# Second layer of a four-layer network: weights and router logits moved into the first layer, the map passes with a PSUM operand, the shared experts as a chain of their own, expert rows added before they are transposed

## The chip, the cores and the metric

The kernel runs on one core of a Trainium2 chip. A core has five engines with queues of their own: TensorE (PE in the profile; its weight loads are listed as PEld), VectorE (DVE), ScalarE (ACT), GpSimd (POOL) and SyncE (SP, which here only issues DMAs). The metric is the device time of one execution in microseconds; lower is better. All arithmetic is fp32.

## What is computed

The network has four layers. Each does `x = x + s * silu(g)`, where s comes from an attention block and g from a feed-forward block, both fed with the layer norm xn of x. There are 8 batches of 512 tokens with 128 features. The change is in the second layer (L1): its s is an RWKV-like recurrence, its g a mixture of experts.

```python
# attention: k, v, r from xn mixed with xn shifted by one token
k = k_in @ Wk;  v = v_in @ Wv;  r = sigmoid(r_in @ Wr)
# per batch and feature, over the 512 tokens:
max_out = maximum(mx, ck + tf)
out = (exp(mx-max_out)*num + exp(ck+tf-max_out)*cv) / (exp(mx-max_out)*den + exp(ck+tf-max_out))
...                                      # mx, num, den decay with td
s = (r * out) @ Wo

# feed-forward: 2 shared experts for every token, and the best 2 of 8 experts
ffn(x, w1, w2, w3) = (silu(x @ w1.T) * (x @ w3.T)) @ w2.T       # 128 -> 256 -> 128
logits = xf @ router_w.T + expert_bias
rw, sel = top_k(logits, 2);  rw = softmax(rw)
g = sum over the two chosen experts of rw * ffn(xf, expert)  +  sum over 2 shared of ffn(xf)
```

The other layers are a windowed attention with a quantised feed-forward (L0), a windowed and latent attention with a phase-weight feed-forward (L2), and a large complex-valued attention with soft experts (L3). L2 needs `tw` (cosine and sine of its phase weights) and `wgg`, which are computed once.

## The kernel before, in words

Activations are kept feature-major: x, xn and s are 128 partitions x 4096 tokens. A batch is one 512-column tile. Engines run what `Net.in_order` records (line 74) in exactly the order of the program, each engine for itself; the profile gives all of these instructions line 83, so groups are told apart by tile names. What is issued without `in_order` may be put anywhere in its engine's queue by the scheduler.

The layer norm of L1 is part of the last steps of L0's feed-forward. That function's order is written out by hand in the string `L0_FFN`: a letter is a step, a number its tile. The steps that matter here are E (centre x on PE), F, G (variance), H (`row`, scaled rows on DVE, also sent to DRAM as `xrows`), I (transpose on PE) and J (`xn` copied by ACT).

After L0, `L2Consts.weights` (line 1198) makes tw and wgg for layer 2: DVE steps on `ang` and `turns`, two Sin on ACT, a small matmul. Then `l1_layer` (line 576) loads its weights by DMA (m1_w13 is 2560 KB, m1_w2 1280 KB), scales its mixing weights `wm` on DVE, and has three stages:

1. `route` (line 758). PE makes the logits `ps_lg` (32 token tiles of 128, 8 columns each), DVE finds the first and second maximum and their one-hot rows (`first_max`), PE counts tokens per expert (`ps_cnt`), and DVE turns the counts into a place for each token and choice. Then eight map passes: DVE compares the place's row with `upto` (0 to 127) to get `ob` (128 x 8 x 128), and its tile with `upto[0:72]` to get `ot` (128 x 8 x 72). POOL and DVE make the two halves of `hold` from ot (token number, gate weight), and PE sums `ps_map` from ob and hold. The result says, for each of 72 tiles of 128 rows, which token stands in each row (`source`) and with which weight. Between logits and maps, the receptances (sigmoid, `ps_mix` into s) are computed for all 8 batches.
2. `tiles` (line 898). For each pair of tiles POOL gathers token rows (`xr`, indirect DMA from xrows), PE transposes them (`tp_g`), multiplies by the pair's expert weights (`ps_ab`, chosen by a register), ACT and DVE make `hh`, PE transposes it (`tp_h`) and multiplies by w2 (`ps_y`); the rows `yy` go to `yrows` in DRAM. Between these, steps of a Python generator `attention` are taken: 19 steps per batch (mixed k and v, scans, one Exp over 128 x 2048 `ex`, four reciprocals, output product `ps_o`), 84 of them in this stage.
3. `rows_back` (line 1001). For each of 8 blocks of 512 tokens, PE computes the shared experts in four parts (`first`: pa and pb with Silu on ACT and the product h on DVE; `second`: accumulate into `acc`). POOL gathers each token's two expert rows (`yr`, 64 indirect DMAs in all); PE turns and adds them into the same accumulator by a matmul with the identity (`back`), 8 per block. Then `gated`: Silu, product with s, sum into x. Attention steps stand between the parts: 10 per block.

PSUM has eight banks. In this layer before: `a1_p` (mixed, ps_o) has 2, `f1_g`, `f1_a` and `f1_t` 2 each.

Of the kernel before, what the change touches and what calls it, by code (L numbers as in the profile page):

```python
# [224 lines left out]
def l0_attention(net, xn, s_out, p0, w, bias):  # L225
# [196 lines left out]
    "B6 I0 F5 E7 D4 J0 C6 G5 E4 F7 H3 D6 I3 F4 G7 E6 J3 G4 F6 H5 G6 I5 H7 J5 H4 I7 H6 I4 "  # L422
    "J7 J4 I6 J6 "
# [3 lines left out]
def l0_ffn(net, x, xn, s):  # L427
    nc, tc = net.nc, net.tc
    K = TB // P
    with ExitStack() as st:  # L430
# [140 lines left out]
        )  # L571
        for part in "".join(L0_FFN).split():
            parts[part[0]](int(part[1:]))


def l1_layer(net, x, xn, s_out):
# [3 lines left out]
    nc, tc = net.nc, net.tc  # L580
    with ExitStack() as st:
        p1 = st.enter_context(tc.tile_pool(name="a1_1", bufs=1))
        p2 = st.enter_context(tc.tile_pool(name="a1_2", bufs=2))
        experts = L1Experts(net, st)
        w = net.load(p1, "a1_w")
        par = net.load(p1, "a1_p")
        td = p1.tile([P, 1], F32, tag="td", name="td")
        nc.scalar.activation(td, par[:, 0:1], AF.Exp)
        nc.vector.tensor_scalar(td, td, -1.0, None, ALU.mult)
        tf = par[:, 1:2]  # L590

        rest = p1.tile([P, 3], F32, tag="rest", name="rest")
        nc.vector.tensor_scalar(rest, par[:, 2:5], -1.0, 1.0, ALU.mult, ALU.add)
        wm = p1.tile([P, 3, 2, P], F32, tag="wm", name="wm")
        for i in range(3):
            nc.vector.tensor_scalar(
                wm[:, i, 0, :], w[:, i, :], par[:, 2 + i : 3 + i], None, ALU.mult
            )
            nc.vector.tensor_scalar(
                wm[:, i, 1, :], w[:, i, :], rest[:, i : i + 1], None, ALU.mult  # L600
            )
# [9 lines left out]
        pp = st.enter_context(tc.tile_pool(name="a1_p", bufs=2, space=PSUM))  # L611
        experts.open_psum(st)
        pe, dve, act, pool = (
            net.in_order(e) for e in (nc.tensor, nc.vector, nc.scalar, nc.gpsimd)
        )

# [9 lines left out]
        def receptance(b):  # L626

            act.activation(s_out[:, ts(b, S)], mixed(2, b), AF.Sigmoid)
# [4 lines left out]
        def attend(b):  # L633
# [48 lines left out]
            dve.tensor_tensor(up, up, out, ALU.mult)  # L682
# [7 lines left out]
        def attention(batches):  # L690
            for b in batches:
                yield from attend(b)

        experts.route(xn, (pe, dve, act, pool), receptance)

        between = attention(range(B))
        experts.tiles((pe, dve, act, pool), between, 84)
        experts.rows_back(x, xn, s_out, (pe, dve, act, pool), between)


class L1Experts:
# [4 lines left out]
    def __init__(self, net, st):  # L706
        nc, tc = net.nc, net.tc
# [54 lines left out]
    def route_in(self, xn, engines, receptance, st):  # L762
# [47 lines left out]
        for b in range(B):  # L810
            receptance(b)
# [1703 lines left out]
```

## Time and profile before

| what | us |
|---|---|
| median of 3 runs (lowest, highest) | 2430.46 (2427.05, 2439.55) |
| the profiled execution, its own time | 2420.28 |
| its span in the trace | 2418.6 |
| PE, DVE, ACT, POOL busy in the span | 2224.3, 2007.3, 1842.5, 1567.8 |

The second layer lies from 403 to 777 us of the span: the first logits matmul starts at 409.57, the first map matmul at 446.36, the first expert matmul at 479.18, the first shared-expert matmul at 638.71, and layer 2's first matmul at 776.77. In a row of the profile's tables, "out<-in" names the tiles written and read; after the bar come busy time and mean duration in ns, then how long the engine stood idle before such instructions and what ended the idleness. An fp32 matmul shows as two records. A matmul's recorded duration overlaps the next one, so the spacing of starts tells its cost.

### The profile page before, as it was taken

Reading aid. Unit: us, or ns where it says so; the run is one execution under the profiler, and the core shown is the slowest. Engines: PE = TensorE matmul, PEld = TensorE weight load, DVE = VectorE, ACT = ScalarE, POOL = GpSimd, SP = SyncE. Lnnn points to the kernel's source line nnn. Section 1 sums busy time; section 2 is a strip of 40 time slices with the busy share of each in tenths; the row PEclk is TensorE's granted clock in tenths of the full one; section 3 lists DMA queues with packets and bytes.
Section 4 is the critical chain, followed back from the end, with each engine's and each line's share of the span. In section 5 each row is a group of like instructions: output and inputs, shape, how many; then the busy total and the mean of one; then the engine's idle time right before and its main releaser. Section 6 shows DMA issues by size and latency. Waiting matters only on the chain.

```text
span 2418.6 us, 49187 instructions
## 1 busy us (share of the span) xinstructions
PE 2224.3 (92%) x17826; PEld 1552.5 (64%) x17826; DVE 2007.3 (83%) x3638; ACT 1842.5 (76%) x3841; POOL 1567.8 (65%) x1422
## 2 busy tenths in 40 slices
PE   6999997689888999868999999999999999999897
PEld 4666675456434666645777777777777777777774
DVE  5577877666675888859999999999999999999474
ACT  4566664155433798947999999999999999999763
POOL 5344434364244878756688788888878878887323
PEclk7899987899999999989999999999999999999888
DMA  2000002022111000033443443344344434433000
GB/s 70 1 2 2 2 1 105 8 63 64 39 29 27 3 16 16 23 111 102 102 112 91 109 114 105 98 102 109 101 110 107 104 91 115 110 91 90 18 1 36
DMA packets 91617, 156.94 MB, mean 65 GB/s; under 512 B 20144, under 2 KB 44464, under 8 KB 91120
## 3 DMA queue, kind: packets, MB, share of 16 engines
q1 hardware_dynamic: 86880, 143.57, 22.5%
q0 software_dynamic: 4352, 8.92, 1.5%
q8 instruction: 142, 2.33, 0.4%
q10 hardware_dynamic: 144, 1.31, 0.1%
q14 instruction: 99, 0.81, 0.1%
HBM read 30.52 MB, written 12.06 MB: 18 GB/s over the span
## 4 chain that ended last, share of the span: by engine, by line
PE 52%; DVE 32%; ACT 5%; POOL 5%; issue 4%; SPq 1%; DMA 1%; POOLq 0%; ACTq 0%; DVEq 0%
PE sc L83 10%; DVE sc L83 7%; DVE y L83 5%; DVE r L83 5%; PE ps_av L83 5%; PE tp L83 4%; PE ps_u L83 4%; PE ps_kq L83 4%; PE av L83 3%; PE ps_n L83 2%; DVE mx L83 2%; PE ps_ab L83 2%; DVE e L83 2%; PE ps_mix L83 2%; PE ps_v L83 1%
## 5 line engine op out<-in xcount | busy, mean ns | idle before, releaser
L83 POOL TENSOR_TENSOR ek<-E,kn 128x512 f32<-128x512 f32 (+3 forms) x512 | 435.0, 872 | 206.7 <-DMA kn<-nr 200.6
L83 PE MATMUL sc<-r 128*128 128x512 f32 (+3 forms) x1024 | 310.1, 446 | 25.3 <-DVE y L83 22.4
L83 POOL TENSOR_TENSOR e<-e,mx 128x1024 f32<-128x1024 f32 x112 | 212.1, 1900 | 182.9 <-DVE mx L83 90.9
L83 POOL TENSOR_TENSOR r<-r,rs 128x1024 f32<-128x1024 f32 x128 | 304.7, 2381 | 21.5 <-DMA rs<-r 21.3
L83 PE MATMUL ps_av<-u,at 128*128 128x128 f32 x2560 | 306.7, 275 | 0.0
L83 PEld LDWEIGHTS ps_av<-u,at 128*128 128x128 f32 x2560 | 296.0, 192 | 0.1
L83 ACT ACTIVATE y<-y,mn 128x384 f32<-128x384 f32 (+3 forms) x512 | 288.8, 569 | 4.0 <-DVE mn L83 3.2
L83 PEld LDWEIGHTS sc<-r 128*128 128x128 f32 x1024 | 165.6, 192 | 190.2 <-issue 120.3
L83 DVE SCALAR_TENSOR_TENSOR y<-sc,qn,V 128x512 f32<-128x512 f32 (+3 forms) x512 | 246.5, 544 | 8.8
L83 DVE CUSTOM_DVE_ANT_0 y<-y,ps_g,ncs 128x384 f32<-128x384 f32 (+3 forms) x512 | 253.2, 541 | 0.0
L83 ACT ACT_TABLE_LOAD x180 | 230.9, 1283 | 10.7 <-PE ps_mix L83 4.3
L83 PEld LDWEIGHTS tp<-ident,y 128*128 128x128 f32 x1280 | 161.7, 142 | 113.3 <-issue 49.3
L83 PE MATMUL tp<-ident,y 128*128 128x128 f32 x1280 | 203.8, 274 | 1.8 <-ACT s L83 0.7
L83 ACT COPY at<-tp 128x512 f32<-128x512 f32 (+1 forms) x384 | 195.3, 509 | 7.8 <-PE tp L83 5.1
L83 DVE TENSOR_TENSOR sc<-sc,EF 128x1280 f32<-128x1280 f32 x128 | 191.9, 1499 | 4.4
L83 DVE SCALAR_TENSOR_TENSOR sc<-sc,ek 128x1280 f32<-128x1280 f32 x128 | 189.7, 1482 | 6.4 <-issue 5.0
L83 POOL TENSOR_TENSOR s<-s,o 128x512 f32<-128x512 f32 x120 | 154.2, 1285 | 32.0 <-ACT o L83 32.0
L83 ACT ACTIVATE y<-y 128x1280 f32<-128x1280 f32 x128 | 163.4, 1277 | 5.0 <-DVE y L83 4.3
L83 DVE TENSOR_TENSOR r<-sn,ps_kq 128x1024 f32<-128x1024 f32 x128 | 155.2, 1212 | 9.6 <-ACT sq L83 9.6
L83 ACT ACTIVATE sq<-ps_kq 128x1024 f32<-128x1024 f32 x128 | 131.7, 1029 | 32.7 <-PE ps_kq L83 32.7
L83 DVE TENSOR_TENSOR r<-ct,ps_kq 128x1024 f32<-128x1024 f32 x128 | 155.2, 1213 | 0.0
L83 ACT ACTIVATE e<-e 128x1024 f32<-128x1024 f32 x112 | 117.3, 1061 | 38.6 <-POOL e L83 38.2
(449 smaller groups left out, 5070.5 us busy)
## 6 DMA issues: line engine op xcount, KB each, us to landing
rs<-r SPq DMA_DIRECT2D x256, 256.0 KB, 3.7
kn<-nr SPq DMA_DIRECT2D x512, 64.0 KB, 2.0
yrows<-yy SPq DMA_DIRECT2D x36, 128.0 KB, 1.8
ct<-trig SPq DMA_DIRECT2D x16, 256.0 KB
EF<-E SPq DMA_DIRECT2D x16, 256.0 KB, 2.4
EF<-E SPq DMA_DIRECT2D x16, 192.0 KB
m_w<-m_w SPq DMA_DIRECT2D x1, 2560.0 KB
x<-x SPq DMA_DIRECT2D x8, 256.0 KB, 5.8
```

What stands on the lines that cost most here:

```text
L83: ins = op(*args, **kwargs)
```

## The change

- **Constants earlier.** A new class `L1Consts` holds L1's weights, masks and counters for the whole of L0 and L1. Four small loads (m1_r, eb, a1_w, a1_p) are issued by SP at the start; the two large ones by ACT's queue ahead of L0's attention. The scalings `wm`, `td`, `rest` are done by ACT there, and the casts of the counters by POOL.
- **Logits in L0.** `L0_FFN` gets steps L (logits of a tile, four matmuls) among its last steps and M (bias added).
- **Layer 2's weights** become a generator, taken as the last steps of `attention`.
- **Receptance** is `tanh(z/2)`; the factors are made up by `(out + 1) * up` and by a Wo scaled with 0.5. Three receptances now stand ahead of ps_cnt on PE, five behind. `a1_p` has one bank (two before).
- **Map passes.** `upto` is copied to PSUM (a bank of f1_g) and both comparisons read it there; ot is made before ob; the gate half of hold is made by ACT, eight scalings per pass. The list of experts (`past`, `ef`) is made after the passes.
- **Shared experts** are a generator `shared_steps` with 32 steps, an accumulator bank `acc` of their own, and their result kept in `sh` (128 x 4096). Four steps stand between map pass 0's operands and its matmuls, one after the maps, one behind the first gathers, eight in the tile loop, the rest in rows_back.
- **Rows** of both choices are gathered into one tile per block (two such tiles), added by DVE (`summed`), transposed by PE (four per block), then `sh` is added on DVE, and Silu and the gate follow, spread over three blocks. Attention steps: 90 in the tile loop, 8 per block afterwards.

```diff
-    "B6 I0 F5 E7 D4 J0 C6 G5 E4 F7 H3 D6 I3 F4 G7 E6 J3 G4 F6 H5 G6 I5 H7 J5 H4 I7 H6 I4 "
-    "J7 J4 I6 J6 "
+    "B6 I0 F5 E7 D4 J0 C6 G5 E4 F7 H3 D6 I3 F4 G7 E6 J3 G4 F6 H5 G6 I5 L0 L1 H7 J5 L2 H4 I7 L3 H6 I4 "
+    "J7 L5 J4 I6 L7 J6 L4 L6 M0 "
...
+        def logits(t):
+            for k in range(K):
+                i = K * t + k
+                pe.matmul(
+                    lg[:, i, :], lhsT=xn[:, ts(i, P)], rhs=router.rw, start=True, stop=True
+                )
...
+class L1Consts:
...
+    def fill(self):
+        net, nc, p1, E = self.net, self.net.nc, self.p1, self.E
+        act = net.in_order(nc.scalar)
+        self.w13 = net.load(p1, "m1_w13", act)
+        self.w2 = net.load(p1, "m1_w2", act)
...
-        pp = st.enter_context(tc.tile_pool(name="a1_p", bufs=2, space=PSUM))
+        pp = st.enter_context(tc.tile_pool(name="a1_p", bufs=1, space=PSUM))
...
-            act.activation(s_out[:, ts(b, S)], mixed(2, b), AF.Sigmoid)
+            act.activation(s_out[:, ts(b, S)], mixed(2, b), AF.Tanh, scale=0.5)
...
-            dve.tensor_tensor(up, up, out, ALU.mult)
+            dve.scalar_tensor_tensor(up, out, 1.0, up, ALU.add, ALU.mult)
...
+            yield from l2.weights(p1, lambda name: pp.tile([P, S], F32, tag="ps", name=name))
...
+    def shared_steps(self):
...
+        def first(b, n):
+            e, j = parts[n]
+            xt = self.xn[:, ts(b, TB)]
+            pa, pb = (self.p_t.tile([P, TB], F32, tag="t", name=n) for n in ("pa", "pb"))
+            pe.matmul(pa, lhsT=w13[:, e, ts(j, P)], rhs=xt, start=True, stop=True)
+            pe.matmul(pb, lhsT=w13[:, e, ts(NH + j, P)], rhs=xt, start=True, stop=True)
+            a = self.p3.tile([P, TB], F32, tag="sa_s", name="sa_s")
+            act.activation(a, pa, AF.Silu)
+            h = self.p3.tile([P, TB], F32, tag="sh_s", name="sh_s")
+            dve.tensor_tensor(h, a, pb, ALU.mult)
+            return b, n, h
+
+        def second(b, n, h):
+            e, j = parts[n]
+            if n == 0:
+                self.acc = self.p_acc.tile([P, TB], F32, tag="acc", name="acc")
+            last = n == len(parts) - 1
+            pe.matmul(self.acc, lhsT=w2[:, e, j, :], rhs=h, start=(n == 0), stop=last)
+            if last:
+                act.copy(self.sh[:, ts(b, TB)], self.acc)
+
+        waiting = None
+        for b in range(B):
+            for n in range(len(parts)):
+                made = first(b, n)
+                if waiting:
+                    second(*waiting)
+                waiting = made
+                yield
+        second(*waiting)
+        yield
...
+        upto = self.p_g.tile([P, P], F32, tag="g", name="upto_p")
+        act.copy(upto, k1.upto)
...
         dve.tensor_tensor(g2, m2, m1, ALU.subtract)
         act.activation(g2, g2, AF.Exp)
-        for b in range(B):
+
+        for b in range(3):
+            receptance(b)
+        cnt = self.p_a.tile([P, 2, NTILE * E], F32, tag="a", name="ps_cnt")
...
+        for b in range(3, B):
             receptance(b)
...
             dve.tensor_tensor(
                 ot, tl[:, cut].unsqueeze(2).to_broadcast(tshp),
-                self.upto[:, 0:NK].unsqueeze(1).to_broadcast(tshp), ALU.is_equal,
+                upto[:, 0:NK].unsqueeze(1).to_broadcast(tshp), ALU.is_equal,
+            )
+            dve.tensor_tensor(
+                ob, at[:, cut].unsqueeze(2).to_broadcast([P, N, P]),
+                upto.unsqueeze(1).to_broadcast([P, N, P]), ALU.is_equal,
             )
...
-            dve.tensor_tensor(
-                hold[:, :, 1, :], ot, val[:, cut].unsqueeze(2).to_broadcast(tshp), ALU.mult
-            )
+            for j in range(N):
+                act.activation(
+                    hold[:, j, 1, :], ot[:, j, :], AF.Copy, scale=val[:, n + j : n + j + 1]
+                )
+            held[n] = ob, hold
...
+        for n in range(0, 2 * NTILE, N):
+            hold_of(n)
             if n == 0:
+                for _ in range(self.A_SHARED - 1):
+                    next(self.shared)
+            add(n)
...
+            def summed(b):
+                dve.tensor_tensor(
+                    rows[b][:, 0], rows[b][:, 0], rows[b][:, 1], ALU.add
                 )
 
             def back(b):
-                for i in range(4 * b, 4 * b + 4):
-                    for c in range(2):
-                        pe.matmul(
-                            acc[b][:, i % 4, :], lhsT=rows.pop((i, c)), rhs=net.ident,
-                            start=False, stop=(i % 4 == 3 and c == 1),
-                        )
+                ps = self.p_g.tile([P, 4, P], F32, tag="g", name="ps_b")
+                r = rows.pop(b)
+                for i in range(4):
+                    pe.transpose(ps[:, i, :], r[:, 0, i, :], net.ident)
+                g = p2.tile([P, TB], F32, tag="sg", name="sg")
+                dve.tensor_tensor(
+                    g, ps.rearrange("p k t -> p (k t)"), self.sh[:, ts(b, TB)], ALU.add
+                )
+                act.activation(g, g, AF.Silu)
+                return g
...
+            for b in range(B + 2):
+                for n in range(3):
+                    if given < left * min(3 * b + n + 1, 3 * B - 3) // (3 * B - 3):
+                        given += 1
+                        next(self.shared, None)
+                    for _ in range(self.C_BETWEEN // 3 + (n < self.C_BETWEEN % 3)):
+                        next(between, None)
+                    if n == 0 and 1 <= b <= B:
+                        summed(b - 1)
+                    if n == 1 and 2 <= b:
+                        gated(b - 2, gs.pop(b - 2))
+                    if n == 2 and 1 <= b <= B:
+                        gs[b - 1] = back(b - 1)
+                        if b + 1 < B:
+                            gather(b + 1)
```

Here `left` is 32 minus the steps already given to the route (A_SHARED = 5) and the tile loop (B_SHARED = 8), and C_BETWEEN is 8.

## The prediction

> **What bounds the kernel now.** First the page's sums, then busy time by stage of the second layer, then the timeline of the stages' seams, then the groups of the last stage. The stages, cut where the chain changes engine (columns: stretch, its length, then busy us and count of PE, PEld, DVE, ACT, POOL, granted clock, DMA share, GB/s):
>
> ```profile
> 403.00:424.00 21.00, 15.39 (x74) 14.81 (x72) 5.59 (x23) 5.90 (x13) 1.63 (x14) 0.64 0.63 238
> 424.00:446.00 22.00, 16.23 (x36) 7.69 (x37) 18.71 (x43) 5.58 (x9) 1.71 (x1) 0.80 0.00 1
> 446.00:474.00 28.00, 17.93 (x130) 16.12 (x128) 21.94 (x23) 0.60 (x1) 11.72 (x8) 1.00 0.00 1
> 474.00:480.00 6.00, 1.85 (x4) 1.01 (x5) 0.00 (x0) 0.37 (x1) 4.64 (x5) 0.77 0.16 44
> 480.00:640.00 160.00, 147.93 (x697) 93.19 (x696) 105.45 (x191) 87.96 (x171) 70.18 (x67) 0.97 0.23 57
> 640.00:777.00 137.00, 116.67 (x352) 56.71 (x351) 88.66 (x125) 45.83 (x61) 67.22 (x64) 0.96 0.13 33
> ```
>
> The layer has 374 us of the 2418.6. PE is nearly full only in the tile loop (480 to 640). Ahead of it the router is a chain that changes engine, behind it PE and DVE wait in turn.
>
> ```profile
> 403.16 0.41 DVE L83 TENSOR_TENSOR ang<-f_w 128x256 f32<-128x256 f32 x1
> 409.57 13.79 PE L83 MATMUL ps_lg<-m_r,xn 128*128 128x8 f32 x64
> 423.40 0.42 DVE L83 TENSOR_TENSOR lg<-ps_lg,eb 128x256 f32<-128x256 f32 x1 [2.36 <-PE ps_lg L83]
> 431.55 0.42 DVE L83 COPY tot<-ps_cnt 128x256 f32<-128x256 f32 x1 [2.13 <-PE ps_cnt L83]
> ...
> 448.52 1.23 DVE L83 TENSOR_TENSOR ob<-at,upto 128x1024 f32<-128x1024 f32 x1 [1.25 <-PE ps_map L83]
> 450.56 1.65 POOL L83 TENSOR_TENSOR hold<-ot,token 128x576 f32<-128x576 f32 x1 [2.27 <-PE ps_map L83]
> 451.12 2.17 DVE L83 TENSOR_TENSOR ob<-at,upto 128x1024 f32<-128x1024 f32 x1
> ```
>
> Layer 2's weights hold 403.2 to 409.5, then the logits 13.8 us at a clock of 0.50. The ob pass takes 1.23 alone and 2.17 while POOL writes hold (450.56 to 452.21), the time that both overlap. One map pass is so 3.55 (ob 451.12, next ob 454.67).
>
> ```profile
> L83 PE MATMUL pa<-xn,m_w 128*128 128x512 f32 x64 | 34.5, 622 | 0.0
> L83 DVE TENSOR_TENSOR h<-a,pb 128x512 f32<-128x512 f32 x32 | 21.4, 671 | 28.4 <-PE pb L83 16.6 <-ACT a L83 11.8
> L83 PE MATMUL acc<-ident,yr 128*128 128x128 f32 x128 | 15.4, 275 | 0.0
> L83 DVE TENSOR_TENSOR x<-x,pr 128x512 f32<-128x512 f32 x7 | 4.8, 692 | 0.2
> ```
>
> In the last stage DVE waits 28.4 for the shared experts' product. A 512-column matmul there is two records that start 0.43 apart, 0.86; a shared step (pa, pb, acc) is 2.57 of PE.
>
> **The sum, part by part** (t is the end of the lg addition, 423.82 before).
>
> Start. The layer's constants come before layer 0. SP issues four loads earlier (0.33 + 0.42 + 0.33 + 0.52); a0_w then goes out at 12.6 for a user at 29.11, so this is covered. The two big loads go out on ACT's queue near 29 us, where the DMA share is 0.02; before, they held the DMA share near 1.0 from 408 to 418, and they are needed after 410. ACT's ten small scalings start 0.2 apart: 2.0, inside ACT's idle 29.06 to 31.18. POOL gets 2.65 or more (iotas 0.67, memsets and selects 1.04, four casts 0.94 by DVE's rows, up to 2.4 by POOL's tt cast of 0.61), and POOL is the chain until rstd at 13.64. Bounds 0 and 4.1; half of the lower sum, since the order is free: **+1.5**.
>
> Logits. After I5 (PE 401.28) PE now has L0 L1 L2 I7 L3 I4 L5 I6 L7 L4 L6. An L is 8 records, 0.13 each at full clock (ps_c), 0.215 at half: 1.04 or 1.72; an I is 0.55. The clock before stayed at 1.00 until 408.7, so I take six L at full clock and two at half: t = 413.1, bounds 412.1 and 415.7. The weights' 6.4 us go out of the way by this too: **-10.7**.
>
> Counts. This is a new wait. ps_cnt now stands behind three receptances; these share one bank (two before), and the first Tanh stands on ACT behind the gate's Exp, which waits for DVE until t+5.7. So: Exp 0.23, Tanh 0.60, mixed 1.72 at full or 3.43 at half clock (2.5), Tanh 0.6, mixed (2.0), cnt 1.8: tot at t+13.6 where it was at t+7.7. DVE's 16 small steps and the map wait behind it: **+5.9**, bounds 4.9 and 7.3 by the two clocks.
>
> The Trainium skill, "TensorE: Matmul & The Clock Gate", Part 1 (What's actually happening), says that the clock halves after one idle window of about 3.4 us and needs as long a busy one to return. Here a gap of 4.9 us (404.1 to 409.0) halved it, as the page has it, but 13.7 us of unbroken logits did not bring it back. By the page the gap of 3.6 us in front of the second receptance is a cold start, and the term would be 7.3.
>
> Map. From tot: on PE five receptances at 1.72 + 0.6 + 0.1 after the first (11.4), four shared steps (12.0, with ACT's table load of 1.28 and hold(0) ahead of the first Silu; DVE's second pass stands behind their four h, so the maps start late by them), eight passes. Per pass DVE has ot 0.75 and ob 1.21, POOL 1.65, ACT eight scalings (two gsel start 0.20 apart at 16 columns, so 0.25 at 72) 2.0, PE 16 x 0.14 = 2.23: PE sets 2.25. That the PSUM operand frees DVE from POOL no row shows outright; if not, 2.92 per pass, +5. Gathers and tp_g follow as before, over two further shared steps. into(0) starts at t+63.0 (before 479.18, tot+47.6): **+1.8**, bounds 0 and 7. So into(0) stands at 476.1, with six of 32 shared steps done.
>
> Tile loop (before 479.2 to 638.6, PE 92% busy). Eight shared steps 20.6, six attention steps of 4.29/19: 1.4. Off: the cold start (two tiles at 0.50), 2.5, and 0.5 where a step falls in PE's wait behind Exp (3.1 each): **+19**, bounds 16 and 24.
>
> Rows (before 638.6 to the last x at 778.2: 139.6). PE falls from 112 to 67: 19 shared steps 48.9, back 32 transposes for 128 records (14.2 to 3.5), attention 14. POOL's 64 gathers at 1.25 stay 80. DVE now leads: 3 batches and a rest at 16.5 each (mx 1.24, num 1.23, den 1.21, four reciprocals 3.7, thirteen of 0.67 to 0.75) 52.8; layer 2's weights 2.9; h 19 x 0.67 = 12.7; sum, add, two for the gate 8 x 2.76 = 22.1: 90.5. Its waits: for Exp 3.89 and 2.16 before, 3.0 x 3; for k 1.1 x 3. The last block, with Sin's and Silu's table loads, 3. The gathers don't decide: the first eight land 3.3 + 10 + 2.5 = 16 us into the stage, where summed(0) stands (a block and 4 us); later ones wait for the transposes two blocks back, as there are two row buffers, and POOL's 10 us a block are under DVE's 11.4 and its waits. In all 106; bounds 94 (no waits), 126 (10.8 a batch as in 691 to 725): **-33.6**.
>
> Tanh for Sigmoid and the merged gate product move table loads and 0.05 a batch: nothing, under the route's waits on PE.
>
> +1.5 - 10.7 + 5.9 + 1.8 + 19 - 33.6 = **-16.1**. The profiled execution took 2420.28 and becomes 2404.2; it lies 10.2 under the median of 2430.46, so the forecast is **2414.4**.
>
> **Rivals.**
> *Denser.* Rows at 94, tiles +16: 15 more, 2399.4. For it: layer 2's steady stage has DVE at 19.7 of 20. Against it: Exp's table loads remain.
> *Moved, not saved.* The shared steps keep their waits, the rows stage takes 126: 2434.4. For it: 28.4 us of DVE's waits belong to h, and they stood on ACT and PE, which still come first. Against it: PE's queue there is 45 us shorter.
> *The cold rows stage, slower.* With PE at 67 of 106 the gate halves the clock in the rows stage. PE then needs 134, 28 more: 2442.4. It decides from a mean clock below 67/106 = 0.63 on. For it: 424 to 432 ran at 0.50 with PE 2.5 of 8 busy. Against it: 676 to 696 kept 1.00 with PE at 14.2 of 20.
> That the change doesn't do what it says is not open for the counts of instructions; only the PSUM operand's effect is, priced above.
>
> **How the numbers follow.** Forecast 0.40 (own range 2405 to 2420), denser 0.22, moved 0.21, cold 0.17. A difference under 0.5% (12 us) can't be told from none. Faster: nearly all of the first two, 0.58. Same: 2418 to 2443 holds moved and part of the cold case, 0.25. Slower: 0.17. The range reaches to 2395 below and 2442 above.
>
> **What would show it.** ps_lg ends by 413 and no layer-2 weights stand ahead of it; tot 13 to 14 us behind lg, with Exp then Tanh as releasers; ob near 1.2 throughout and ps_map unbroken; tile loop near 178; rows stage near 106 with DVE busy about 90 and a clock over 0.9. The forecast is wrong if the rows stage stays over 120, or if the tile loop takes more than its 22 us of added PE work.

## The result, and the profile after

The changed kernel takes 2439.96 us (median of 13 runs, 2430.77 to 2444.61) where the kernel before takes 2430.01 on the same chip: a ratio of 1.0039, 95% interval 1.0022 to 1.0055. So it is slower by 0.4%, about 10 us, and the prediction of 16 us less was wrong in its sign. The profiled execution took 2444.1 us, with a span of 2441.2. It lies 4 above its median, while the profiled execution of before lies 10 under its own, so the two traces differ by 22.6 us and the medians by 10. A second trace of each, taken on other chips, has spans of 2436.6 (changed) and 2437.9 (before): whole traces scatter by more than the change is worth, so what follows compares the lengths of stages.

Behind layer 2's first `row` both traces need the same time (1637.8 and 1636.7 us), so everything happens up to there. Busy time by stage of the second layer in the changed kernel (columns: stretch, its length, then busy us and count of PE, PEld, DVE, ACT, POOL, granted clock, DMA share, GB/s; the stages are logits, counts, receptances and four shared steps, maps, first gathers, tile loop, rows):

```profile
403.00:416.00 13.00, 13.00 (x81) 12.54 (x79) 2.91 (x7) 3.80 (x6) 1.07 (x2) 0.67 0.26 81
416.00:433.00 17.00, 13.07 (x20) 5.14 (x18) 5.67 (x15) 1.91 (x4) 0.00 (x0) 0.55 0.01 1
433.00:458.00 25.00, 19.30 (x40) 7.62 (x39) 10.63 (x26) 8.62 (x18) 1.15 (x1) 0.93 0.00 0
458.00:475.00 17.00, 17.00 (x132) 16.29 (x131) 15.31 (x22) 13.86 (x56) 8.06 (x7) 1.00 0.01 2
475.00:486.00 11.00, 5.82 (x15) 2.55 (x15) 1.37 (x2) 2.52 (x5) 7.95 (x9) 0.84 0.15 42
486.00:673.00 187.00, 169.02 (x735) 103.41 (x735) 116.14 (x204) 94.90 (x180) 69.35 (x64) 0.95 0.18 47
673.00:797.00 124.00, 84.69 (x189) 35.44 (x189) 88.35 (x131) 39.36 (x58) 65.29 (x64) 0.83 0.13 36
```

The maps are now what the change wanted, PE busy in 17.00 of 17. But DVE, which was to lead the rows stage, works there for 88.35 us of 124: 36 us are waits.

The timeline at the same seams as before (start, duration, then idle time before it and what ended that):

```profile
415.25 0.42 DVE L83 TENSOR_TENSOR lg<-ps_lg,eb 128x256 f32<-128x256 f32 x1 [10.03 <-PE ps_lg L83]
432.19 0.42 DVE L83 COPY tot<-ps_cnt 128x256 f32<-128x256 f32 x1 [10.92 <-PE ps_cnt L83]
...
458.08 16.04 PE L83 MATMUL ps_map<-hold,ob 128*128 128x144 f32 x128
...
460.56 1.22 DVE L83 TENSOR_TENSOR ob<-at,upto_p 128x1024 f32<-128x1024 f32 x1
460.81 1.15 POOL L83 TENSOR_TENSOR hold<-ot,token 128x576 f32<-128x576 f32 x1 [0.73 <-ACT hold L83]
```

The lg addition stands 8 us earlier than before, tot does not: 16.9 us lie between them (8.2 before). ob takes 1.22 even while hold runs, and hold 1.15 where it was 1.65.

The groups that answer to pa and h of before (h is now called sh_s, Silu's result sa_s; busy time, mean ns, then idle time before them by releaser; over the whole layer):

```profile
L83 PE MATMUL pa<-xn,m_w 128*128 128x512 f32 x64 | 37.0, 663 | 8.9 <-ACT sa_s L83 8.9
L83 DVE TENSOR_TENSOR sh_s<-sa_s,pb 128x512 f32<-128x512 f32 x32 | 21.8, 681 | 48.2 <-ACT sa_s L83 24.7 <-PE pb L83 23.5
```

DVE's idle time in front of the shared experts' product is 48.2 us over the layer, where it was 28.4. In the rows stage alone, DVE waits for (us in total, times, longest):

```profile
DVE sh_s L83 <- ACT sa_s L83: 13.6, 8, 3.3
DVE sh_s L83 <- PE pb L83: 13.2, 3, 6.8
```

So 26.8 us, though PE's queue is shorter there; moving 13 of the 32 steps away took only 1.6 us of these waits with it (4.2 in the second trace, where they are 24.2).

### The profile page after: what moved, and what is told of

It reads as the page before. It is cut to its first block, busy times and chain, and to the rows that moved or that the text cites. A ratio compares the mean times of both kernels' runs of the same rounds, so it can differ in the third digit from the quotient of the medians.

```text
span 2441.2 us, 49058 instructions
## 1 busy us (share of the span) xinstructions
PE 2221.3 (91%) x17730; PEld 1537.6 (63%) x17730; DVE 2002.6 (82%) x3634; ACT 1862.5 (76%) x3921; POOL 1565.0 (64%) x1426
## 4 chain that ended last, share of the span: by engine, by line
PE 34%; DVE 23%; POOL 4%; ACT 4%; issue 3%; DMA 2%; SPq 1%; POOLq 0%; ACTq 0%; DVEq 0%
PE sc L83 8%; DVE sc L83 7%; DVE r L83 6%; DVE y L83 6%; PE ps_av L83 5%; PE ps_u L83 4%; PE ps_kq L83 4%; PE tp L83 3%; PE ps_n L83 2%; SPq L1975 1%; PE ps_p L83 1%; POOL ek L83 1%; DMA rs<-r 1%; POOL r L83 1%; POOL e L83 1%
## 5 line engine op out<-in xcount | busy, mean ns | idle before, releaser
L83 PE MATMUL sc<-r 128*128 128x512 f32 (+3 forms) x1024 | 311.1, 447 | 26.8 <-DVE y L83 23.7
```

Source lines behind the costliest of these rows:

```text
L83: ins = op(*args, **kwargs)
```

## The experiments

Each kernel was timed beside the kernel before on one chip; ratios are to that, with 95% intervals. The table gives stage lengths from each trace, as differences of start times: the lg addition, the cast to `source`, the first ps_ab, the last yy, the last x of layer 1, the first `row` of layer 2. The last yy stands for the end of the tile loop in all of them, since shared steps no longer mark it.

| run | ratio to before | lg to source | to ps_ab | to last yy | to last x | to row | sum |
|---|---|---|---|---|---|---|---|
| before, first trace | | 48.9 | 6.9 | 162.7 | 135.6 | 3.3 | 357.4 |
| before_again | 0.9996 (0.9976-1.0015) | 48.9 | 7.0 | 172.4 | 135.8 | 3.3 | 367.4 |
| changed, first trace | 1.0039 (1.0022-1.0055) | 58.9 | 11.4 | 190.2 | 121.1 | 7.7 | 389.3 |
| again | 1.0051 (1.0036-1.0066) | 59.0 | 11.4 | 184.4 | 118.1 | 7.7 | 380.6 |
| list_early | 1.0049 (1.0032-1.0067) | 59.1 | 9.2 | 189.2 | 118.4 | 7.7 | 383.5 |
| pa_bank | 1.0047 (1.0030-1.0063) | 60.0 | 11.3 | 184.9 | 118.4 | 7.7 | 382.4 |
| fill_late | 1.0030 (1.0011-1.0049) | 60.2 | 11.3 | 184.9 | 117.9 | 3.6 | 377.9 |
| cnt_first | 1.0057 (1.0037-1.0077) | 59.2 | 11.4 | 184.3 | 118.0 | 7.7 | 380.6 |
| late_out | 1.0014 (1.0001-1.0027) | 58.8 | 11.4 | 181.8 | 114.5 | 7.7 | 374.3 |
| attn_early | 1.0142 (1.0121-1.0164) | 56.6 | 11.4 | 224.5 | 99.6 | 7.7 | 399.7 |
| turn_add | 1.0035 (1.0020-1.0049) | 60.1 | 11.4 | 185.2 | 121.4 | 7.7 | 385.8 |
| no_head_steps | 1.0004 (0.9988-1.0021) | 45.6 | 9.4 | 183.8 | 124.1 | 7.7 | 370.6 |
| shared_late | 1.0060 (1.0034-1.0086) | 60.0 | 11.5 | 170.0 | 134.9 | 7.7 | 384.1 |
| all_late | 1.0048 (1.0031-1.0064) | 46.0 | 9.3 | 170.0 | 146.8 | 7.7 | 379.8 |
| all_late_mended | 0.9996 (0.9978-1.0014) | 46.1 | 9.4 | 168.9 | 143.4 | 3.6 | 371.3 |
| upto_sbuf | 1.0071 (1.0045-1.0096) | 62.7 | 11.3 | 186.3 | 120.5 | 7.7 | 388.6 |
| logits_last | 1.0051 (1.0032-1.0070) | 60.2 | 11.4 | 189.3 | 118.0 | 7.7 | 386.6 |
| mended | 0.9961 (0.9944-0.9978) | 46.0 | 9.3 | 185.5 | 121.2 | 3.6 | 365.6 |
| mended_banks | 0.9966 (0.9950-0.9981) | 46.0 | 9.3 | 180.5 | 119.3 | 3.6 | 358.6 |
| mended_all | 0.9957 (0.9940-0.9974) | 46.1 | 9.2 | 180.4 | 124.6 | 3.6 | 364.0 |

### Both kernels once more

> The kernel before as it is, for a second trace. If the first trace (2420.28 us, at the low end of its runs) is typical in layer 1: 355 to 360 us from the lg addition to layer 2's first row (357.4), with 49, 163 and 136 from lg to the first source cast, first ps_ab to last yy, and last yy to last x. If layer 1 was short by chance in that execution: 363 to 368. Time as before's other runs, ratio 1.000 within 0.002.

> The changed kernel as it is, so that the others are compared with it on one chip, and so that a second trace shows which of its stalls return. From the first source cast to the first ps_y it took 29.8 us in the first trace and 23.9 to 24.7 in three kernels that leave this stretch as it is; if the 5 us were of that one execution, 24 to 25 here, and 378 to 384 us from the lg addition to layer 2's first row (389.3 in the first trace). If they belong to the kernel, 29 to 30 again. Time 2428 to 2434 where the kernel before takes 2422.

The layer took 367.4 us in before's second trace, 10 more than in the first, all of it in the tile loop; the changed kernel's second trace lacks 8.7 of its first (5.8 of them in the tile loop). The other stages agree within 0.2 us for before, and within about 3 for the changed kernel. So the tile loop's length has to be compared as a range, 162.7 to 172.4 before and 184.4 to 190.2 after, and a rows stage between 118.1 and 121.1 is not told apart from the changed kernel's.

### Counts first, and the list of experts early

```diff
-        for b in range(3):
-            receptance(b)
         cnt = self.p_a.tile([P, 2, NTILE * E], F32, tag="a", name="ps_cnt")
...
-        for b in range(3, B):
+        for b in range(B):
             receptance(b)
```

> The changed kernel, with ps_cnt ahead of all eight receptances on PE (three stand ahead of it now). Theory 'counts', as in the prediction: ps_cnt's wait is on the path that sets the end; tot stands 8 us behind lg (16.6 now), the maps and all behind them come 5 to 8 us earlier, and so does the end. Rival 'PE's work is the path': DVE's operands for the first pass are ready at 441.6, but PE has eight receptances and four shared steps ahead of the maps in either order; the first pa then moves by under 2 us from 28.5 behind lg, or later if the receptances now run cold, and the time changes by under 2.

The timeline of this kernel at the lg addition, tot and the first pa:

```profile
415.38 0.42 DVE L83 TENSOR_TENSOR lg<-ps_lg,eb 128x256 f32<-128x256 f32 x1 [9.88 <-PE ps_lg L83]
423.94 0.42 DVE L83 COPY tot<-ps_cnt 128x256 f32<-128x256 f32 x1 [2.55 <-PE ps_cnt L83]
...
444.56 1.02 PE L83 MATMUL pa<-xn,m_w 128*128 128x512 f32 x2
```

tot comes 8.6 behind lg instead of 16.9, and nothing follows: the first pa stands 29.2 behind lg (28.8 in the changed kernel), and the ratio is no better. The rival holds in its outcome: eight receptances and the shared steps are ahead of the maps in either order, and the wait that the prediction priced at 5.9 us is off the path. It is not PE's work alone, though: two things cancel here. PE stands idle for 6.1 us in front of ps_cnt, and the receptances behind it run at full clock (1.00 from 424.8 to 436) where the first three of the changed kernel ran at half.

In list_early `past`, `ef` and `expert` are made right behind the first pass's operands.

> The changed kernel, with the list of experts (past, ef, expert) made behind the first map pass's operands, as before the change, and not after the last pass. Theory 'register loads': PE stands 3.1 us (482.5 to 485.5) in front of the first ps_ab because two loads of expert numbers into its registers come there, and more of them come between the first tiles; with the list made early some of them move into PE's idle time before the maps. First ps_ab then 6 to 9 us behind the source cast (11.4 in the changed kernel, 6.9 before), first ps_y 22 to 25 behind it (29.8; 19.4 before), the time 5 to 8 us below the changed kernel's. Rival 'cold seam': the stall is the gathers' latency and a PE at clock 0.58; then the first ps_ab comes no more than 3 us earlier, first ps_y too, and the time changes by under 2 us.

The first ps_ab moves up by 2.2 us, within the rival's 3, and PE's gap ahead of it falls from 3.1 to 1.0: that much the register loads cost there. The tile loop gives it back (189.2, within its range), and the time shows nothing.

### Layer 2's fills

`vw` and `gv` are filled by POOL memsets whose program text the change does not touch. In the changed kernel's timeline they stand between layer 1's last x and layer 2's first row:

```profile
796.77 0.69 DVE L83 TENSOR_TENSOR x<-x,sg 128x512 f32<-128x512 f32 x1
...
797.66 1.90 POOL L1259 MEMSET vw<- 128x2160 f32 x1 [10.72 <-PE ps_c L83]
...
803.43 1.04 POOL L83 TENSOR_TENSOR std<-var,neg_half 128x4 f32<-128x4 f32 x1
804.50 0.69 DVE L83 TENSOR_TENSOR row<-ps_c,std 128x512 f32<-128x512 f32 x1 [5.61 <-POOL std L83]
```

```diff
                 pool.tensor_tensor(self.std[n], v, net.neg_half.to_broadcast([P, K]), ALU.pow)
+                k.fill_now(pool)
```

`fill_now` holds the memsets of vw and gv and runs once.

> The changed kernel, with layer 2's fills of vw and gv (eight POOL memsets, 5.4 us) put behind the first std of layer 2. Before the change they ran at 8 to 16 us of the span; in the changed kernel they run at 797.7 to 803.1, since the memory of vw is now used in layer 1, and POOL makes the first std behind them. Theory 'memory': from the last x of layer 1 to the first row of layer 2 it is 7.0 us now and was 2.6; it becomes 2.6 to 3.2 again, and the time falls by 4 to 4.5 us, as POOL stands idle for 5.3 us behind the first std. Rival: the fills then delay kbs or vw of the first batch and the 4.4 us are given back there; the time changes by under 1.5.

In fill_late's timeline:

```profile
790.37 2.61 POOL L83 MEMSET vw<- 128x2160 f32 x3
790.43 0.69 DVE L83 TENSOR_TENSOR row<-ps_c,std 128x512 f32<-128x512 f32 x1 [1.44 <-POOL std L83]
```

From the last x to the first row it takes 3.6 us instead of 7.7, so 4.2 us come back; the ratio moves about as far (0.0021 below again's), but the two intervals overlap, so that the trace shows this gain and the time does not. That the memory of vw is reused is read from the wait (the fill waits for layer 1's end; before, it ran at 8.3 us of the span); the addresses themselves were not looked at.

### What the rows stage waits for

pa_bank: `pa` of a shared step in f1_a's banks while rows are brought back, `pb` in f1_t as it was.

> The changed kernel, with pa of a shared step in the two banks of f1_a while rows are brought back (they stand idle there); pb stays in f1_t. Theory 'two banks': pa and pb of one step fill both banks of f1_t, so PE can't begin the next step before DVE has taken h, and DVE's 26.8 us of waits in front of sh_s in this stage (13.6 for ACT's sa_s, 13.2 for PE's pb) come from that. They fall under 14, and the stage from the last yy to the last x from 121.8 to 107 to 112; the time 10 to 14 us below the changed kernel's. Rival 'the list of work on DVE and ACT': sh_s waits because Exp with its two table loads stands ahead of Silu on ACT, and PE because the reciprocals stand ahead of h on DVE; more banks move the waits to other tiles, and the stage falls by 4 at most.

PE's waits in the rows stage of pa_bank:

```profile
PE ps_o L83 <- DVE up L83: 19.0, 4, 10.6
PE acc L83 <- DVE sh_s L83: 12.1, 8, 4.1
```

The stage stays at 118.4: the rival holds. PE no longer waits in front of pa and pb, and waits instead in front of acc for DVE's h (12.1, where it was 4.4 in the changed kernel) and, above all, as before, in front of ps_o, for `up` at the end of DVE's reciprocals (15.8 in the changed kernel). What stands in PE's queue behind ps_o waits too.

```diff
-            ps = pp.tile([P, S], F32, tag="ps", name="ps_o")
-            pe.matmul(ps, lhsT=w[:, 3, :], rhs=up, start=True, stop=True)
-            act.copy(out, ps)
...
             act.copy(v, mixed(1, b))
             yield
+            product_of_last_batch()
```

`product_of_last_batch` is the three lines taken out, for the batch before; batch 7 keeps them where they were.

> The changed kernel, with ps_o of an attention batch issued behind the next batch's k and v instead of two steps behind up (the last batch's as it was). Theory 'ps_o blocks PE': in the rows stage PE stands up to 10.6 us in front of ps_o until DVE has done the reciprocals and up, with the next shared step's pa and pb behind it, and DVE then waits for pb: that is why 26.8 us of DVE's waits stand in front of sh_s. PE's wait for up falls from 16 to 19 us to under 6, DVE's waits for sh_s to under 14, and the stage from the last yy to the last x from 118 to 105 to 111; the time 7 to 13 us below the changed kernel's. Rival 'DVE's own list': what PE gains at ps_o it loses in front of acc, as h stands behind the same reciprocals on DVE; the stage falls by 3 at most.

PE's largest wait in late_out's rows stage:

```profile
PE ps_o L83 <- DVE up L83: 10.8, 1, 10.8
```

What is left in front of ps_o is the one wait of the last batch, which has no next batch to hide behind. DVE's waits for sh_s fall only to 21.5 (11.4 + 10.1; 24.2 in again), the stage to 114.5, the tile loop by 2.6 (inside its spread), and the ratio to 1.0014: 9 us less than again on the same chip, with intervals that don't touch. So ps_o was part of it; the theory's 105 to 111 for the stage is not reached, and the banks (pa waits 7.3 for sa_s) come up next. They are tried together below.

turn_add lets PE add the two rows again (eight matmuls with the identity per block, no sum on DVE).

> The changed kernel, with the two gathered rows added by PE again: per block eight matmuls with the identity into ps_b instead of DVE's sum and four transposes. So DVE has 8 x 0.68 = 5.4 us less and PE some 64 records more (3.5 to 7 us by the clock). Theory 'DVE leads the rows stage', as in the prediction: the stage from the last yy to the last x falls from 118 by 3 to 6. Rival 'waits lead it': neither DVE's 5.4 nor PE's 7 stands on the path; it changes by under 2. If it grows by 3 or more, adding on DVE was worth it.

The stage takes 121.4: 3.3 more than in again, but no more than the 121.1 of the changed kernel's first trace, and the time (1.0035 against 1.0051) doesn't part them either. It does not fall by 3 to 6, so DVE's 5.4 us of work are not what the stage hangs on; what adding on DVE is worth is not shown.

### Where shared steps and attention stand

```diff
-    B_BETWEEN = 90
+    B_BETWEEN = 128
```

> The changed kernel, with 128 steps of attention in the tile loop where it has 90, so 24 and layer 2's weights are left for the rows stage instead of 62. Theory 'rows stage follows DVE and its waits': two batches of 16.5 us of DVE and their waits for Exp and ps_o leave it: 118 to 82 to 92, held by POOL's 64 gathers at 1.25; the tile loop, bound by PE, grows by 38 steps of 4.29/19, 8.6, or up to 14 with new waits: time 12 to 25 us below the changed kernel's. Rival 'moved': the tile loop's PE waits for the denser attention as much as the rows stage sheds, or the gathers hold the rows stage at 105; the time changes by under 6.

The rows stage sheds 18.5 us and the tile loop gains 40, 1.05 per attention step where PE's work is 0.23. Neither theory holds: the loop takes more than the rows stage sheds, and the kernel is some 22 us slower than again. In the loop PE now waits 15.8 us in front of ps_ab for DVE (3.0 in the changed kernel) and 7.6 in front of ps_y for ACT (2.4), which with 8.6 of work names 27 of the 40. The tile loop is bound by PE only while its other queues are loose.

```diff
-    A_SHARED = 5
+    A_SHARED = 1
```

> The changed kernel, with one shared step in the route where it has five: none stands between the first pass's operands and the maps, and the four go to the rows stage. From the first pa to the first map matmul it took 14.0 us (10.3 of PE and a wait of 3 for Silu's table). Theory 'the rows stage has room': the maps start 31 to 33 us behind the lg addition instead of 42.9, the first source cast 47 to 49 (59.0), and the stage from the last yy to the last x grows from 118 by no more than 5 (four h of 0.68 and some waits): time 6 to 11 us below the changed kernel's. Rival 'a shared step costs as much there': with 3 us for each it grows by 12, and the time changes by under 3.

The theory holds, with both sizes a little past its ranges: 13.4 us less up to `source`, 2 less to the first ps_ab, and 3.0 to 6.0 more in the rows stage (against the changed kernel's two traces). The ratio of 1.0004 is some 10 us under the changed kernel's. A shared step ahead of the maps cost 3.8 us of the path; in the rows stage it costs 1.5 or less.

shared_late has B_SHARED = 0 instead of 8, all_late has both edits, all_late_mended also those of late_out and fill_late. With more than 21 steps left the rows stage gives one or two at each place (`while given < ...` for `if`).

> The changed kernel, with none of the shared steps in the tile loop (eight now) and 27 in the rows stage (19 now), one or two at each of its places. Theory 'the rows stage has room': from the first ps_ab to the last yy 184.4 becomes 162 to 166 (eight steps of 2.57), and the rows stage grows from 118 by 5 to 10: time 10 to 16 us below. Rival 'a shared step costs as much there': the rows stage grows by 16 to 24, as DVE waits for each sh_s, and the time changes by under 4.

> The changed kernel, with one shared step in the route and none in the tile loop, so that 31 of the 32 stand in the rows stage, nearly as before the change. Theory 'the rows stage has room': both savings add up, 12 from the route and 20 from the tile loop, against 8 to 15 more in the rows stage (118 to 126 to 133; it was 135.6 before the change): time 17 to 24 us below the changed kernel's, under that of the kernel before by 5 to 12. Rival 'a shared step costs as much there': the rows stage goes to 145 or more, and the time is within 5 of the changed kernel's.

> As all_late, with ps_o behind the next batch's k and v, and layer 2's fills behind its first std. Theory: both gains found alone (9 by the time or 6 by the trace, and 4.2) add to that of all_late: 10 to 13 us below all_late, and 15 to 25 below the kernel before. Rival: with 31 shared steps in the rows stage PE's wait for up is filled already by them, so that of the two only the fills' 4 us remain.

Here the rival holds: eight steps leave the tile loop (-14.4) and cost 16.9 in the rows stage, 2.1 each; in all_late against no_head_steps 22.7 for 13.8. The rows stage has room for four more steps, not for twelve. The mended one gains 12 us on all_late, as the theory has it, and yet only reaches the kernel before: with 31 steps there, the rows stage loses what the route and the tile loop gain.

### Two parts of the change alone

In logits_last the steps L0 to L7 follow J6 in the list, ahead of M0.

> The changed kernel, with the logits of all eight tiles behind the last step of the first layer (behind the last xn) instead of between its last steps. Theory, as in the prediction's logits term: 32 narrow matmuls then stand on the path, 8.3 us at full clock and 13.8 at half; less the 2 to 4 that stand there now: the lg addition 6 to 10 us behind where it is, and the time 5 to 9 us above the changed kernel's. Rival: the logits between the last steps delay the transposes and xn by what they take, so the place is worth nothing: time within 3.

The rival holds: ratio 1.0051, again's own. In this trace the last xn is copied at 402.1 (410.3 in the changed kernel), and the lg addition follows 9.4 us later, at 411.5 (4.9 later there): as the time is the same, logits among the last steps seem to push xn back by what they take, though single positions scatter by more than this (see the end). The trace shows one thing more. The 64 records of logits run from 401.9 to 411.4 without a gap, and in their midst the granted clock halves (stretch, its length, busy us and count by engine as above, clock, DMA share, GB/s):

```profile
402.00:406.40 4.40, 4.40 (x42) 4.40 (x41) 0.00 (x0) 1.97 (x3) 0.00 (x0) 1.00 0.36 112
406.40:411.40 5.00, 5.00 (x26) 5.00 (x25) 0.00 (x0) 0.00 (x0) 0.00 (x0) 0.50 0.00 0
```

In upto_sbuf the map passes read upto from SBUF.

> The changed kernel, with upto read from SBUF in the map passes instead of PSUM. Theory 'the PSUM operand frees DVE from POOL': ob takes about 2.2 us again where POOL's hold overlaps it (1.21 to 1.22 now), hold 1.65 on POOL (1.15 now); a pass is then 0.75 + 2.2 of DVE instead of PE's 2.0, and from the first map matmul to the source cast it takes 21 to 25 us instead of 16.1: time 5 to 8 us above the changed kernel's. Rival 'ACT taking the gate half frees it': DVE no longer makes a half of hold, and ob stays at 1.2 to 1.3; the maps stay under 18, the time within 2.

A map pass of it, and the next one's ot:

```profile
459.88 1.21 DVE L83 TENSOR_TENSOR ob<-at,upto 128x1024 f32<-128x1024 f32 x1
460.13 1.97 POOL L83 TENSOR_TENSOR hold<-ot,token 128x576 f32<-128x576 f32 x1 [0.79 <-DVE ot L83]
461.02 1.70 DVE L83 TENSOR_TENSOR ot<-tl,upto 128x576 f32<-128x576 f32 x1
```

The maps take 21.8 us instead of 16.1, as the theory has it, but the slow pass is now ot (1.70 for 0.75), since it is ot that starts while hold runs, and hold grows from 1.15 to 2.0. From lg to `source` the kernel loses 3.7 us of the 5.7, as the four shared steps ahead of the maps took 12.5 in this trace and not 14.0. The ratio of 1.0071 agrees with the theory, but its interval reaches down to again's ratio.

### The faults taken away

mended joins no_head_steps, late_out and fill_late; mended_banks adds pa_bank; mended_all also moves layer 2's weights behind batch 6.

> The changed kernel, with one shared step in the route (four moved to the rows stage), ps_o behind the next batch's k and v, and layer 2's fills behind its first std. Theory: what the three gave alone adds up, 11 (time, no_head_steps), 6 to 9 (late_out) and 4 to 5 (fill_late): 21 to 25 us below the changed kernel's 2435, which is 2410 to 2414 where the kernel before takes 2424, ratio to before 0.994 to 0.996; from lg to layer 2's first row 358 to 362 (380.6). Rival: late_out and no_head_steps fill the same PE wait, and together give 12: ratio 0.998 to 1.000.

> As mended, with pa in the two idle banks of f1_a in the rows stage. Theory 'the causes mask each other': alone the banks gave nothing, as ps_o held PE anyway; now PE's waits of 10.9 for sh_s in front of pb and 8.9 for sa_s in front of pa fall to under 8 together, DVE's waits for sh_s from 25.5 to under 17, and the stage from the last yy to the last x from 121 to 110 to 116: time 5 to 10 us below mended, ratio to before 0.992 to 0.994. Rival 'DVE's list': what PE does earlier then waits in front of acc for h, which stands behind the reciprocals; the stage falls by 2 at most, the ratio stays at 0.995 to 0.997.

> As mended_banks, with layer 2's weights behind the attention of batch 6 instead of batch 7. In mended their seven steps on DVE (2.9 us) and four on ACT stand between the last batch's product and the last two blocks' sums; theory: the last x then comes 2 to 3 us earlier, the time 2 to 3 below mended_banks. Rival: the last batch's attention moves back by the same 2.9 and is the end of the chain itself: no change, within 1.

mended is faster than both kernels: ratio 0.9961, 9.4 us under the kernel before on its chip and some 20 under the changed one (0.0084 below the mean of its two ratios). The gains add up, a little short of the theory's low end (21); from lg to layer 2's first row it takes 365.6, not 358 to 362. More banks again give nothing that the time can show, and the waits move on; in mended_banks, of PE:

```profile
PE acc L83 <- DVE sh_s L83: 18.2, 13, 3.6
```

and of DVE:

```profile
DVE sh_s L83 <- PE pb L83: 14.1, 4, 4.3
DVE sh_s L83 <- ACT sa_s L83: 11.4, 7, 3.7
```

25.5 us in front of sh_s, as in mended. The rival "DVE's list" holds as to what more banks give. Why it holds is read from the traces and not shown by a run: h stands behind the reciprocals on DVE, Silu behind Exp on ACT, and pa, Silu, h and acc of a step are issued at one place on each engine. A step whose h is issued a place later was not tried. mended_all (0.9957) is not told apart from mended_banks: in its trace the rows stage is even longer (124.6), with 9.2 us before sg for ps_b.

## Why the prediction was wrong, step by step

Set against means of the two traces of each kernel (and for the first line of all 16 executions whose work ahead of it is that of the changed kernel):

| step of the sum | forecast | measured |
|---|---|---|
| start and logits: the lg addition | -9.2 | 417.0 - 426.3 = -9.3 |
| counts and map: lg to first ps_ab | +7.7 | 70.3 - 55.8 = +14.5 |
| tile loop | +19 | 187.3 - 167.6 = +19.7 |
| rows | -33.6 | 119.6 - 135.7 = -16.1 |
| last x to layer 2's row | 0 | 7.7 - 3.3 = +4.4 |
| sum | -16.1 | +13.2 |

The medians' ratios say +9.5 and +12.4 us, so the steps account for the result within their scatter.

**Rows** is the step that failed, by 17.5 us. Its work was right (DVE 90.5 forecast, 88.35 measured); its waits were not. The sum gave them 15.3 us (3.0 x 3 for Exp, 1.1 x 3 for k, 3 for the last block) and none to h, which had 28.4 before, in the belief that a shorter PE queue removes them. Measured are 34.4 us of DVE's waits in this stage, 26.8 of them for h. PE and DVE take turns there. One such turn in the changed kernel:

```profile
748.65 0.69 DVE L83 SCALAR_TENSOR_TENSOR up<-s,up 128x512 f32<-128x512 f32 x1
749.49 2.05 PE L83 MATMUL ps_o<-up,a_w 128*128 128x512 f32 x2 [3.01 <-DVE up L83]
751.33 1.91 PE L83 MATMUL pa<-xn,m_w 128*128 128x512 f32 x2
753.04 1.92 PE L83 MATMUL pb<-xn,m_w 128*128 128x512 f32 x2
755.06 0.69 DVE L83 TENSOR_TENSOR sh_s<-sa_s,pb 128x512 f32<-128x512 f32 x1 [5.11 <-PE pb L83]
```

PE stands idle in front of ps_o until DVE has done the reciprocals and up; then it works through ps_o, pa and pb, and DVE waits for pb. The other long wait for pb (6.8 us, ended at 688.8) follows a ps_o in the same way. For sa_s, DVE's waits of 3.3 and 1.9 us come behind ACT's Exp and the table load after it, and four of 1.2 behind the gate's Silu, which stands ahead of the step's own Silu on ACT and itself waits for DVE's sum (9.7 us once). Only the part of ps_o is shown by a run (late_out: 3.6 us of the stage against again, 9 of the time); the rest is read from this trace, and with ps_o out of the way 25.5 us of waits for h remain (mended_banks), and what would remove them stays open. The same stretch and the tail show what else was missed (740 to 750, then 750 to 756, then from 774 on):

```profile
740.00:750.00 10.00, 4.37 (x12) 1.72 (x11) 8.66 (x13) 1.12 (x2) 7.13 (x7) 0.77 0.16 46
750.00:756.00 6.00, 6.00 (x8) 2.21 (x7) 0.69 (x1) 1.18 (x2) 1.12 (x2) 0.54 0.08 25
...
774.00:797.00 23.00, 8.45 (x25) 5.01 (x24) 20.73 (x35) 4.48 (x12) 8.16 (x9) 0.50 0.09 26
```

While DVE does reciprocals PE idles, and then works at a clock of 0.54 with DVE idle (0.69 of 6). From 774 on all shared steps are done and DVE runs the last batch, layer 2's weights and the last sums nearly alone: before the change the shared experts stood in that tail, and attention had ended.

Of the rivals, "moved, not saved" comes nearest as a mechanism: it named these waits and took 126 for the stage, 20 more than the forecast's 106; measured is 17.5 more as a change and 13.6 more as a length (119.6 from the last yy). The cold rival's time (2442.4) lies nearer to the measured 2439.96, but by luck: the rows stage has a mean clock of 0.83, and that rival needed less than 0.63. Half clock came in pieces there (mean 0.66 from 683 to 688 and from 707 to 712, 0.53 from 745 to 756, 0.51 from 772 on).

**Counts and map** were 7 us too low, just past their two upper bounds together. From lg to the first pa it took 28.8 (25.4 by the working), for the four shared steps 14.0 (12.0), for the maps 16.1 (18), from source to ps_ab 11.4 (8, the rest of the 63). The first is the clock: all three receptances ran at half (3.76 to 3.78 for a mixed, where 2.5 and 2.0 were taken), and tot came 8.8 us later behind lg than before (16.94 against 8.15), past the term's upper bound. (That term's items add up to 13.4 and not 13.6, and with both mixed at half to 15.8, which makes the bound 8.1 and not 7.3.) The prediction weighed here the rule of the Trainium skill, "TensorE: Matmul & The Clock Gate", Part 1 (What's actually happening), that an idle window of about 3.4 us halves the clock, and looked at the gap in front of the second receptance. The clock had fallen before that gap: from 407 to 415 its mean was 0.53 with PE busy for 8.00 of 8, on the last transposes and logits, and it stayed at 0.50 until 431.3, through the first receptance too. logits_last shows it fall in the midst of logits alone. That matmuls of 8 columns by themselves let the clock fall is the nearest reading; no run varied their width.

"DVE's 16 small steps and the map wait behind it" is false as a cost of the path: in the changed kernel ACT has made its half of the first hold by 446.8 and PE starts the maps at 458.1, and cnt_first gains nothing by an earlier tot. And the four shared steps ahead of the maps were costed fairly but seen as neutral; they were the dearest place for them.

**Layer 2's fills** were in no term: they are in no line of the diff. A tile whose memory layer 1 now uses can be filled only behind layer 1.

**Tile loop**: the +19.7 lies near the forecast's +19, but single pairs of traces give 12.0 to 27.5, so the runs don't contradict the term, but hardly confirm it. **PSUM operand**: upto_sbuf shows the 5 us that the prediction set against it (5.7 measured in the maps). The Trainium skill, "SBUF — State Buffer", SBUF: two separate sides, says that DVE with two SBUF inputs and POOL take one port pair in turns, each for a whole instruction; the rows agree, as ot starts 0.9 us into hold's 1.97 and ends 0.62 after it.

**Start and logits** came out at -9.3 for -9.2, and that closeness is luck: the lg addition moves by 15 us between executions of the same work, and before has only two traces (423.4 and 429.1). At a like clock (mean 0.92 from 25 to 380 us in before's first trace and in cnt_first) it comes 8 us earlier, and no run parts the start's +1.5 from the rest. What earns, by the traces, is what the term named: layer 2's weights out of the way (403.2 to 409.5 before) and logits that run partly at full clock instead of 0.50. Their place among layer 0's steps earns nothing that the time shows (logits_last).

## What to carry to other kernels

A wait is not removed by shortening one of the queues it passes: find the instruction that stands in front of it in every queue (here ps_o in PE's; Exp and the gate's Silu in ACT's and the reciprocals in DVE's, as the trace has them), and leave the waits of before in the sum until one of them is named as gone. Price a piece of movable work by the path at each place where it may stand: one shared step cost 3.8 us ahead of the maps, 1.8 in the tile loop, and up to 1.5 for four and 2.1 to 2.8 for eight more in the rows stage. After a change that holds memory for longer, look in the trace for what else moved, fills and loads above all, also where no line was edited.

## What the runs showed that was not expected

The lg addition stood anywhere from 410.4 to 425.8 us in 16 executions with the same work ahead of it. Layer 0 takes that, with its granted clock: from 25 to 380 us the mean was 0.94 in pa_bank (410.4) and 0.88 in all_late_mended (425.8). Some of it fell while PE was busy throughout. From 260 to 300 us, in again and then in all_late_mended:

```profile
260.00:300.00 40.00, 38.40 (x520) 25.40 (x522) 31.05 (x38) 25.98 (x42) 18.93 (x10) 1.00 0.01 2
```

```profile
260.00:300.00 40.00, 39.26 (x416) 25.06 (x415) 24.96 (x31) 20.45 (x33) 14.54 (x8) 0.77 0.00 1
```

The one has a clock of 1.00 and 520 records, the other 0.77 and 416, with PE busy for 39.26 of 40. In the latter the clock fell between 240 and 250, after ten microseconds in which PE was busy for 10.00 of 10, so no idle gap explains it, and it stays open what does. Also open is a stall in the tile loop, mostly near its start, that both kernels show in some executions: in before's second trace PE waits in front of ps_ab three times, 6.5 us in all, for nothing that the profile names, and its tile loop is 10 us longer; in the changed kernel's first trace it is 7.6 us.
